# Two layers of attention and feed-forward on one core: who copies the last weight fold behind a branch, when Silu's table is loaded, and where two leftover value products stand

## The chip, the cores and the metric

The kernel runs on one core of a Trainium2 chip. The metric is the device time of one execution in microseconds (us), as the median over runs. The engines are named PE (TensorE), DVE (VectorE), ACT (ScalarE), POOL (GpSimd) and SP (SyncE, which issues most of the transfers).

## The reference

The input `x` is 8 x 100 x 512 and the context 8 x 361 x 128, all in float32. Two layers follow each other, each with an attention over the context and a feed-forward part:

```python
x = x + L0_xattn(layernorm(x), ctx)   # 16 heads of 32, causal mask, softmax
x = x + L0_ffn(layernorm(x))          # 8 experts, the best 2 per token, silu(x W1) * (x W2) W3
x = x + L1_xattn(layernorm(x), ctx)   # latent attention, 16 heads, rotated context, softmax over 361
x = x + L1_ffn(layernorm(x))          # weights, rows and hidden rounded to 8-bit steps, silu(gate) * up
```

In the second layer's attention the queries go through three weight matrices, `Wq`, `w_kc_q` and `W_qr`. They depend on no token, so the kernel multiplies them with each other once.

## The kernel before

The 800 tokens stand in seven tiles of 128 rows (the last has 32). The program is one long list of instructions for each engine. In most of it the order on PE, DVE and ACT is the order in which the program is written (`manual_schedule`); SP's and POOL's transfers are put in by a scheduler, which may also move them across a piece of code.

**The fold.** The product of the three weight matrices, `wqf`, is made in eight pieces, one for each pair of heads, beside the routing of the first layer. A piece goes through four steps: `fold_first` (two pieces at a time, small matmuls), `fold_turn` (two transposes by PE into a bank of PSUM, and a copy back into SBUF, L786), `fold_second` (matmuls with `Wq`, and a copy into the tile `f_p`, L796) and `fold_third` (four transposes of `f_p`, L802, and a copy into `wqf`, L803). All these copies are ACT's. The last pair of pieces is called `u4`: its `fold_first` and `fold_turn` stand ahead of the branch, its `fold_second` and `fold_third` behind it.

**The branch.** Each expert takes 240 tokens at most. If an expert has more, a slow loop of its own handles the rest; with these inputs it isn't entered. Each engine loads the flag `spilt` into a register (L1002) and skips the loop (L1009). Ahead of the branch POOL issues two indirect transfers that gather the rows of the first expert's tokens (`first_rows`, L906). On the skipped side POOL waits until both have landed and then raises the counters of its transfer queues by what the loop would have added; after that it gathers the rows of the second and third expert (`xg`).

**Behind the branch.** The order written out is: `fold_second` of both pieces of `u4`, `fold_third` of the first, `columns_of` (transposes of the gathered rows, L1128, in two parts of 128 and 112 rows; ACT copies the first part into `xgT`, L1132, DVE the second, L1130), `fold_third` of the second piece, and then the experts. An expert's matmuls of gate and up (L1191) read `xgT`. ACT applies Silu to the gate (L1202). A one-element Silu at L930, written into a corner of the tile `sd0`, stands at the end of the part ahead of the branch, so that the function's table is loaded early. `sd0` lies in a pool that is closed right behind it; the space is used again by the tiles into which SP loads the second layer's feed-forward weights (`gu`, L947, 256 KB each, and `dn`, L952, 704 KB), which DVE rounds beside the experts.

**The second layer's attention.** The work is cut into halves `(b, h)` of a batch, each with six tiles (`HT` is 6). A tile is a step: `scores(n)` (a matmul on PE, L1497, the row maximum `nm` on DVE, L1502, the exponential on ACT, L1505, into one of four buffers `e`), `scaled` (POOL divides by the sum, L1515) and `turned_squares` (DVE transposes squares of 32 x 32 into `sq`, L1522). Behind the six steps stands `values` of the half before (96 matmuls on PE, L1531, into the tile `four`, which takes four banks of PSUM and exists once).

Of 100 query rows 96 fit these tiles. The leftover rows of two batches and all heads make one tile of their own; it has its scores behind an even batch, and is finished in the second half of the next batch: `rest_columns` at step 2 (three transposes, L1546, into `four`, copied by ACT, L1548 and L1549) and `rest_values` at step 4 (six matmuls, L1558, into `four` again, copied by ACT into `ctxT`, L1563). A function put at a step by `at_step` is called ahead of this step's `scores`. There are four such halves.

Of the kernel before, what the change touches and what calls it, by code (L numbers as in the profile page):

```python
# [15 lines left out]
AF = mybir.ActivationFunctionType  # L16
# [3 lines left out]
P = 128  # L20
# [30 lines left out]
def tile_kernel(  # L51
# [7 lines left out]
    nc = tc.nc  # L59
# [19 lines left out]
    def bank(dtype=F32):  # L79
        cols = 512 if dtype == F32 else 1024  # L80
        bank_turn[0] += 1
        pool = bank_pools[bank_turn[0] % len(bank_pools)]
        return pool.tile([P, cols], dtype, tag="bank", name="bank")
# [15 lines left out]
    ln_eps = keep.tile([P, 1], F32, tag="ln_eps", name="ln_eps")  # L99
# [142 lines left out]
    sd0 = at.tile([P, NT], F32, tag="sd0", name="sd0")  # L242
# [527 lines left out]
    def fold_first(t_p, *pairs):  # L770
        pa = bank()
        for n, (i, wq_p, kq_p, qr_p) in enumerate(pairs):
            for c in range(CQ // P):
                for j in range(2):
                    nc.tensor.matmul(
                        pa[ds(R1 * j, R1), ts(n, P)], qr_p[:, j, c, :], kq_p[:, j, c, :],
                        start=(c == 0), stop=(c == CQ // P - 1),
                    )
        nc.scalar.copy(t_p, pa[:, : 2 * P])
        return [(i, wq_p) for i, wq_p, _, _ in pairs], t_p  # L780

    def fold_turn(pairs, t_p):
        pa = bank()
        for n in range(2):
            nc.tensor.transpose(pa[:, ts(n, P)], t_p[:, ts(n, P)], ident)
        nc.scalar.copy(t_p, pa[:, : 2 * P])  # L786
        return [(i, wq_p, t_p[:, ts(n, P)]) for n, (i, wq_p) in enumerate(pairs)]

    def fold_second(i, wq_p, a_p):
        pb = bank()  # L790
        for j in range(2):
            nc.tensor.matmul(
                pb[ds(R1 * j, R1), :], a_p[:, ts(j, R1)], wq_p[:, j, :], start=True, stop=True
            )
        f_p = fw.tile([P, D], F32, tag="f_p", name=f"f_p{i}", bufs=2)
        nc.scalar.copy(f_p, pb)  # L796
        return i, f_p

    def fold_third(i, f_p):
        pt = bank()  # L800
        for c in range(KC):
            nc.tensor.transpose(pt[:, ts(c, P)], f_p[:, ts(c, P)], ident)  # L802
        nc.scalar.copy(wqf[:, :, ts(i, P)], pt.rearrange("p (c r) -> p c r", c=KC))  # L803
# [43 lines left out]
    turned = at.tile([P, 2, 2 * P], F32, tag="zeros", name="turned")  # L847
    turned = [turned[:, 0], turned[:, 1]]
# [11 lines left out]
    token_scales(mvs, sd_all, rstd_all, 5, 7)  # L860
    u2 = fold_first(turned[1], loaded.pop(0), loaded.pop(0))
    u1 = fold_turn(*u1)
    nc.scalar.activation(sd0[:, 0:1], ln_eps, AF.Exp)
    for t in range(5, 7):
        gate_norm(t)
    mark_places(0, 5)
    u3 = fold_first(turned[2], loaded.pop(0), loaded.pop(0))
    u2 = fold_turn(*u2)
    f0 = fold_second(*u1[0])
    xT = gate_columns(5, 7)  # L870
    u3 = fold_turn(*u3)
    f1 = fold_second(*u1[1])
    name_tokens(0, 5)
    for i in (6, 7):
# [3 lines left out]
    add_tokens(0, 5)  # L878
    fold_third(*f1)
    f0 = fold_second(*u2[0])  # L880
    rank_choices(5, 7)
    f1 = fold_second(*u2[1])
# [10 lines left out]
    turned = fw.tile([P, 2 * P], F32, tag="a_p", name="turned3", bufs=1)  # L893
    u4 = fold_first(turned, loaded.pop(0), loaded.pop(0))
# [7 lines left out]
    def gather(e, tiles):  # L902
        got = []
        for i, xg in enumerate(tiles):
            n = SLOTS[i][1]
            d = nc.gpsimd.indirect_dma_start(  # L906
                out=xg, out_offset=None, in_=x_rows,
                in_offset=bass.IndirectOffsetOnAxis(
                    ap=token_of[:n, 2 * e + i : 2 * e + i + 1], axis=0
                ),  # L910
            )
            got.append((xg, d.ins))
        return got
# [7 lines left out]
    slots = {0: gather(0, first_rows)}  # L921
    most = small.tile([P, 1], F32, tag="most", name="most")
# [2 lines left out]
    nc.vector.tensor_scalar(spilt, most, float(CAP), None, ALU.is_gt)  # L925
    f3 = fold_second(*u3[1])
    fold_third(*f2)
    u4 = fold_turn(*u4)
    fold_third(*f3)
    nc.scalar.activation(sd0[:, 0:1], ln_eps, AF.Silu)  # L930
    close_atw()
    close_at()

# [174 lines left out]
    def choices(e, got):  # L1108
        gates = []
        for i, (xg, _) in enumerate(got):  # L1110
            n = SLOTS[i][1]
            one = ffw.tile([P, 1], F32, tag="one", name=f"one{e}_{i}", bufs=4)[:n]
            nc.vector.tensor_scalar(one, xg[:, D + 2 : D + 3], float(NE - e), None, ALU.is_equal)
            gate = ffw.tile([P, 1], F32, tag="gate", name=f"gate{e}_{i}", bufs=4)[:n]
            nc.vector.scalar_tensor_tensor(
                gate, xg[:, D : D + 1], one, xg[:, D + 1 : D + 2], ALU.mult, ALU.add
            )
            place = small.tile([P, 1], I32, tag="place", name=f"place{e}_{i}")[:n]
            nc.vector.tensor_copy(place, xg[:, D + 3 :])
            gates.append((gate, place))  # L1120
        return gates

    def columns_of(e, got):
        xgT = ffw.tile([P, KC, CAP], F32, tag="xgT", name=f"xgT{e}")
        for i, (s0, n) in enumerate(SLOTS):
            pt = bank().rearrange("p (c q) -> p c q", c=KC)
            for c in range(KC):
                nc.tensor.transpose(pt[:, c, :n], got[i][0][:, ts(c, P)], ident[:n, :n])  # L1128
            if i % 2:
                nc.vector.tensor_copy(xgT[:, :, ds(s0, n)], pt[:, :, :n])  # L1130
            else:
                nc.scalar.copy(xgT[:, :, ds(s0, n)], pt[:, :, :n])  # L1132
        return xgT
# [41 lines left out]
    )  # L1175
    in_order.__enter__()

    folded = [fold_second(*a) for a in u4]
    fold_third(*folded[0])
    turned = columns_of(0, slots[0])  # L1180
    fold_third(*folded[1])
    gates = choices(0, slots[0])

    for e in range(NE):
# [44 lines left out]
        if e + 1 < NE:  # L1229
            turned = columns_of(e + 1, slots[e + 1])  # L1230
# [18 lines left out]
        for m, i in down:  # L1249
            mr = HCH[m][1]  # L1250
            s0, n = SLOTS[i]
# [4 lines left out]
        for i in range(HC):  # L1256
            gate, place = gates[i]
            n = SLOTS[i][1]
# [181 lines left out]
    pairs, kvrs, kvTs, kv4s = {}, {}, {}, {}  # L1440
# [153 lines left out]
    for g, tiles in enumerate(GROUPS):  # L1594
        xT = xT_next
        n = sum(ROWS[t] for t in tiles)
# [52 lines left out]
    def at_step(k, i, f, *args):  # L1649
        beside.setdefault((k, i), []).append(lambda: f(*args))  # L1650

    for b in range(B):
        k = 2 * b
        at_step(k, 1, context_blocks, b, 0)
        at_step(k + 1, 0, context_blocks, b, 1)
        if b + 1 < B:
            at_step(k + 1, 0, next_columns, b + 1)
        if b % 2 == 0:
            at_step(k + 1, 0, next_rows, b)
            q = (k - 2, k) if b > 2 else (0, 1)  # L1660
            if b:
                for h in range(2):
                    at_step(q[h], 2 if q[h] else 5, queries, b, h, copies)
        else:
            n = first_of[b] - 1
            at_step(k + 1, 2, rest_columns, n)
            at_step(k + 1, 4, rest_values, n)

    turning = []

# [3 lines left out]
    for k, (b, h) in enumerate(halves):  # L1674
        n0 = first_of[b] + HT * h
        behind_rest = h == 0 and b % 2 == 1
        for i in range(HT):
            n = n0 + i
# [18 lines left out]
        if h and b % 2 == 0:  # L1697
            n = n0 + HT
# [364 lines left out]
```

## Time and profile before

| | |
|---|---|
| median of 3 runs | 624.99 us (624.87 to 627.96) |
| the profiled execution | 624.9 us, its span 622.7 us |
| granted TensorE clock, mean | 0.997 |
| PE busy (matmuls) | 601.0 us, 97% of the span |
| DVE, ACT, POOL busy | 403.5, 231.8, 238.8 us |
| the branch and what stands behind it, to the first expert's matmul | 132.8 to 140.2 us |
| experts | 140.2 to 261.3 us |
| second attention, steps and values | 321 to 484 us |

The span runs from the first to the last instruction; 2.2 us of the execution lie around it. Line numbers are those of the kernel before. A name such as `first_rows` or `four` is that of a tile in the program. In a row of a timeline the figures are the start, the duration, the engine, the line, the operation, the tiles, and in brackets the idle time of the engine ahead of it with the engine that ended it.

### The profile page before, as it was taken

Reading aid. Unit: us, or ns where it says so; the run is one execution under the profiler, and the core shown is the slowest. Engines: PE = TensorE matmul, PEld = TensorE weight load, DVE = VectorE, ACT = ScalarE, POOL = GpSimd, SP = SyncE. Lnnn points to the kernel's source line nnn. Section 1 sums busy time; section 2 is a strip of 40 time slices with the busy share of each in tenths; the row PEclk is TensorE's granted clock in tenths of the full one; section 3 lists DMA queues with packets and bytes.
Section 4 is the critical chain, followed back from the end, with each engine's and each line's share of the span. In section 5 each row is a group of like instructions: output and inputs, shape, how many; then the busy total and the mean of one; then the engine's idle time right before and its main releaser. Section 6 shows DMA issues by size and latency. Waiting matters only on the chain.

```text
span 622.7 us, 12244 instructions
## 1 busy us (share of the span) xinstructions
PE 601.0 (97%) x4587; PEld 399.4 (64%) x4594; DVE 403.5 (65%) x1041; ACT 231.8 (37%) x533; POOL 238.8 (38%) x242
## 2 busy tenths in 40 slices
PE   8999999979999999999999999999999999999995
PEld 5767765647777777658877677777777544444442
DVE  4865778836777554253227888788874366766687
ACT  3553545561111111241336545556553121222130
POOL 1131231021333332208954868688685001222020
PEclk9999999999999999999999999999999999999998
DMA  8900096558999999773623332433210401110221
GB/s 279 326 20 35 2 298 182 179 155 255 306 301 268 233 329 308 201 197 102 180 67 86 91 101 53 127 88 88 59 50 6 139 10 32 24 31 11 53 41 68
DMA packets 92932, 83.75 MB, mean 134 GB/s; under 512 B 41195, under 2 KB 69567, under 8 KB 92743
## 3 DMA queue, kind: packets, MB, share of 16 engines
q1 hardware_dynamic: 88775, 73.57, 41.3%
q0 software_dynamic: 4096, 9.38, 7.3%
q8 instruction: 37, 0.61, 0.4%
q14 instruction: 24, 0.20, 0.1%
HBM read 63.75 MB, written 12.36 MB: 122 GB/s over the span
## 4 chain that ended last, share of the span: by engine, by line
PE 69%; DVE 5%; ACT 2%; issue 1%; POOL 1%; ACTq 0%; DVEq 0%
PE bank L390 13%; PE bank L1191 12%; PE four L1531 11%; PE bank L1497 8%; PE bank L1614 7%; PE bank L1252 7%; PE bank L1789 3%; PE bank L1292 2%; PE four L1461 2%; PE bank L1128 1%; PE four L1558 1%; ACT e L1505 1%; DVE sq L1522 1%; POOL hid L1806 1%; PE bank L396 1%
## 5 line engine op out<-in xcount | busy, mean ns | idle before, releaser
L1515 POOL TENSOR_SCALAR e<-e,rs 128x361 f32<-128x361 f32 x96 | 113.0, 1192 | 41.1 <-DVE rs L1511 40.8
L390 PE MATMUL bank<-wvo,ctxT 128*128 128x512 f32 x192 | 84.4, 594 | 0.0
L1505 ACT ACTIVATE e<-bank,nm 128x361 f32<-128x361 f32 x100 | 56.5, 567 | 51.6 <-DVE rs L1511 43.5
L1191 PE MATMUL bank<-xgT,w 128*128 128x240 f32 (+1 forms) x384 | 74.1, 369 | 0.4 <-ACT xgT L1132 0.4
L1191 PEld LDWEIGHTS bank<-xgT,w 128*128 128x128 f32 (+1 forms) x384 | 64.7, 181 | 11.5 <-issue 6.2
L1502 DVE TENSOR_REDUCE nm<-bank 128x1 f32<-128x361 f32 x100 | 50.8, 509 | 27.1 <-PE bank L1497 19.0
L1531 PEld LDWEIGHTS four<-sq,kv 32*128 32x128 f32 (+1 forms) x1536 | 62.2, 185 | 8.4 <-issue 4.8
L1497 PE MATMUL bank<-kvT,qe 128*128 128x361 f32 x192 | 67.3, 483 | 0.2
L1531 PE MATMUL four<-sq,kv 32*128 32x192 f32 (+1 forms) x1536 | 66.9, 325 | 0.0
L1806 POOL TENSOR_TENSOR hid<-g,u 128x512 f32<-128x512 f32 (+1 forms) x17 | 20.4, 1216 | 112.1 <-ACT g L1797 110.5
L390 PEld LDWEIGHTS bank<-wvo,ctxT 128*128 128x128 f32 x192 | 36.0, 190 | 42.5 <-issue 41.8
L1522 DVE STREAM_TRANSPOSE sq<-e 128x384 f32<-128x384 f32 x96 | 53.6, 558 | 1.6 <-POOL e L1515 0.8
L1264 POOL DMA_INDIRECT x_acc<-y,place x16 | 25.1, 1570 | 75.6 <-ACT y L1263 45.1
L355 POOL TENSOR_TENSOR s<-s,rs 100x800 f32<-100x800 f32 x16 | 24.4, 1522 | 70.3 <-DVE rs L354 35.5
L1497 PEld LDWEIGHTS bank<-kvT,qe 128*128 128x128 f32 x192 | 33.4, 189 | 22.6 <-issue 5.7
L1252 PE MATMUL bank<-w,hT 128*128 128x512 f32 (+3 forms) x96 | 42.6, 593 | 0.0
L1614 PE MATMUL bank<-xT,wqf 128*128 128x256 f32 (+1 forms) x128 | 31.2, 394 | 0.0
L1252 PEld LDWEIGHTS bank<-w,hT 128*128 128x128 f32 (+3 forms) x96 | 17.0, 183 | 19.7 <-issue 15.6
L1789 PE MATMUL bank<-w1q,xqT 128*128 128x512 bf16 (+1 forms) x140 | 29.2, 361 | 0.2
L1614 PEld LDWEIGHTS bank<-xT,wqf 128*128 128x128 f32 x128 | 23.8, 190 | 5.3 <-issue 0.5
L1794 DVE SCALAR_TENSOR_TENSOR g<-bank,sx,swb 128x512 f32<-128x512 f32 (+1 forms) x18 | 12.6, 702 | 19.0 <-PE bank L1789 18.5
L1202 ACT ACTIVATE silu<-bank 128x240 f32<-128x240 f32 x16 | 5.9, 370 | 50.1 <-PE bank L1191 50.1
(296 smaller groups left out, 961.5 us busy)
## 6 DMA issues: line engine op xcount, KB each, us to landing
w<-in_w SPq DMA_DIRECT2D x8, 1408.0 KB
gu<-in_wgu SPq DMA_DIRECT2D x22, 256.0 KB
wq_p<-in_wq SPq DMA_DIRECT2D x8, 512.0 KB
w<-in_w SPq DMA_DIRECT2D x16, 256.0 KB
wo<-in_wo SPq DMA_DIRECT2D x8, 512.0 KB
kq_p<-in_wkcq SPq DMA_DIRECT2D x16, 192.0 KB
kv<-ctx_rot SPq DMA_DIRECT2D x32, 96.0 KB
dn<-in_wdn SPq DMA_DIRECT2D x4, 704.0 KB
```

The source lines that it names most:

```text
L390: nc.tensor.matmul(po[:, :D], lhs[:, c, ds(t * P, r)], rhs[:, c, :], start=(c == 0), stop=(c == chunks - 1),)
L1191: nc.tensor.matmul(po, w12_e[:, c, cols], xgT[:, c, :], start=(c == c0), stop=(c == c1 - 1))
L1252: nc.tensor.matmul(py[i][:n], hT[:mr, m, ds(s0, n)], w3_e[:mr, m, :], start=(m == blocks[0]), stop=(m == blocks[2]),)
L1497: nc.tensor.matmul(ps[:, :L], of_batch(b)[a][:, h, s].rearrange("p g q -> p (g q)"), kvTs[b], start=True, stop=True,)
L1502: nc.vector.tensor_reduce(nm, ps[:, :L], AX.X, ALU.max, negate=True)
L1505: nc.scalar.activation(e[:, :L], ps[:, :L], AF.Exp, bias=nm, accum_out=sm)
L1515: nc.gpsimd.tensor_scalar_mul(e[:, :L], e[:, :L], rs)
L1522: nc.vector.transpose(squares[b, h][:, a * (HT // 2) + s, :], e)
L1531: nc.tensor.matmul(pc[:, g, :cols].rearrange("p (t q) -> p t q", q=32), kv4s[b, j // NBH][ds(32 * g, n), j % NBH, :], eT[ds(32 * g, n), :, ...
L1614: nc.tensor.matmul(pq[:, i, :], wqf[:, c, ts(p0 + i, P)], xT[:, c, :], start=(c == 0), stop=(c == KC - 1),)
L1789: nc.tensor.matmul(pw[:r, :n], xqT[:, c, :r], w1q[:, c, ds(off, n)], start=(c == 0), stop=(c == KC - 1),)
L1806: nc.gpsimd.tensor_tensor(hid[:r, ds(c0, n)], g[:r, :n], u[:r, :n], ALU.mult)
```

## The change

It has three parts.

1. `fold_turn` of `u4` and the first `fold_second` of `u4` get DVE's copy instead of ACT's.
2. The one-element Silu goes from the end of the part ahead of the branch to the start of the part behind it, and writes `most` (a small tile that is not in the closed pool) instead of `sd0`. The second piece's `fold_third` goes between the two parts of `columns_of`.
3. `rest_values` goes from step 4 to step 5.

```diff
-    def fold_turn(pairs, t_p):
+    def fold_turn(pairs, t_p, copy=nc.scalar.copy):
...
-        nc.scalar.copy(t_p, pa[:, : 2 * P])
+        copy(t_p, pa[:, : 2 * P])
...
-    def fold_second(i, wq_p, a_p):
+    def fold_second(i, wq_p, a_p, copy=nc.scalar.copy):
...
-        nc.scalar.copy(f_p, pb)
+        copy(f_p, pb)
...
-    u4 = fold_turn(*u4)
+    u4 = fold_turn(*u4, nc.vector.tensor_copy)
     fold_third(*f3)
-    nc.scalar.activation(sd0[:, 0:1], ln_eps, AF.Silu)
...
-    def columns_of(e, got):
+    def columns_of(e, got, between=lambda: None):
...
         for i, (s0, n) in enumerate(SLOTS):
+            if i:
+                between()
...
-    folded = [fold_second(*a) for a in u4]
+    nc.scalar.activation(most, ln_eps, AF.Silu)
+    folded = [fold_second(*u4[0], nc.vector.tensor_copy), fold_second(*u4[1])]
     fold_third(*folded[0])
-    turned = columns_of(0, slots[0])
-    fold_third(*folded[1])
+    turned = columns_of(0, slots[0], lambda: fold_third(*folded[1]))
...
-            at_step(k + 1, 4, rest_values, n)
+            at_step(k + 1, 5, rest_values, n)
```

In the built program the order on the engines changes in these places, and in two more on SP's queue. The first two `gu` loads stand ahead of SP's branch, where they stood behind it: the tiles that they fill no longer wait for ACT's Silu in `sd0`. And in the second attention, one load of rotated context columns (`kvT`) stands ahead of the second part of a load of context rows (`kvr`), three times. On ACT there is one table load behind the branch, where there were two (ahead of L786's copy and at L930). DVE's copy of L786 stands ahead of DVE's branch.

## The prediction

> **What bounds the kernel now.** PE's matmuls fill 97% of the span, so a change pays only where PE stands idle, or where its work gets shorter (none does here). I first read the chain that ended last around the branch. From 133.7 to 137.8 us it isn't on PE:
>
> ```profile
> 133.70 1.28 ACT L786
> ...
> 135.00 0.37 ACT turned L786
> 135.37 0.49 ACT wqf L803
> ...
> 135.86 1.28 ACT L930
> ...
> 137.36 0.48 ACT f_p L796
> ...
> 137.89 0.66 PE bank L802 x4
> 138.54 0.82 PE bank L1128 x8
> 139.37 0.44 PE bank L802 x4
> ...
> 140.18 1.86 PE bank L1191 x8
> ```
>
> ACT loads a table, copies, loads the next table, and PE's last fold hangs on it. The timeline of PE gives what PE lost: 1.20 us at the branch itself, 0.95 ahead of L792 (for `turned`), 0.53 ahead of L802 (for `f_p`), 0.38 ahead of L1191 (for `xgT`). The change is aimed at the 0.95 and the 0.53.
>
> Next the transfers there, in the timeline of POOL and the two tiles' views (from issue to landing):
>
> ```profile
> 131.27 1.23 POOL L906 DMA_INDIRECT first_rows<-x_rows,token_of  x1 [31.90 <-DVE spilt L925]
> 132.81 0.96 POOL L906 DMA_INDIRECT first_rows<-x_rows,token_of  x1 [0.31 <-PE bank L802]
> 138.56 0.96 POOL L906 DMA_INDIRECT xg<-x_rows,token_of  x1 [4.79 <-PE bank L802]
> ...
> DMA to landing us min/median/max: 4.6/4.6/4.6
> ...
> DMA to landing us min/median/max: 5.8/6.4/6.7
> ```
>
> The first rows landed at 131.27 + 4.6 = 135.9 and 132.81 + 4.6 = 137.4, the later gathers (`xg`) took 5.8 to 6.7. Third, SP's waits there and DVE's queue ahead of its `xgT` copy (the view of L1130):
>
> ```profile
> SPq L947 <- ACT sd L930: 4.9, 1, 4.9
> ...
> L1130 DVEq EVENT_SEMAPHORE  x8: 49/50/1064, 137.7 to 138.3; - x8
> ```
>
> SP held the `gu` loads 4.9 us for the Silu into `sd0`. DVE's eight waits ahead of L1130 begin at 137.7, just behind the second landing: POOL raises its queues' counters only then. Last, the waits of the second attention:
>
> ```profile
> PE four L1558 <- ACT rest L1549: 2.3, 4, 0.6
> ```
>
> Four times PE stands 0.45 to 0.62 us for the copies of the leftover columns.
>
> **The branch, on PE.** PE's first matmul behind it stays at 133.96: DVE's new copy waits for PE's transposes (over at 132.5) and takes at most the 0.62 of L1130's larger copy, so it ends by 133.2; behind it on DVE stand only the branch and a copy that isn't wanted before 135.4. Three L802 end at 134.47. `turned` is ready, so L792 follows at once: eight instructions in 1.94 us, half of them at 135.45 and all at 136.42. DVE's copy of `f_p` is priced by L1296 (128x512 out of PSUM, 0.69): over at 136.2, under the second half. Then four L802 (0.66) to 137.1, four transposes of rows (half of 0.98) to 137.5, four L802 (0.44) to 138.0, four transposes to 138.4. ACT's copy of the second `f_p` (0.58, from 136.5) is covered, and so is its one table load (133.7 to 135.0). What the new order costs: DVE's `xgT` copy (0.62) now stands behind the last transposes with no L802 over it, and with the hand-overs on both sides (0.1 each) L1191 starts at 139.2. Sum: 140.18 - 139.2 = 1.0 us won, 0.95 + 0.53 less some 0.45.
>
> **The branch, on the transfers.** There is a second way to L1191. From the second landing to DVE's first wait it is 0.26, the other seven waits take 0.78 (0.1 each) up to the copy, then 0.62 and 0.1: landing plus 1.8. With 137.4 that is 139.2 too. So behind the change both ways end together, and each tenth by which the gather lands later is lost on PE.
>
> It will land later. With the Silu out of `sd0`, the `gu` loads don't wait, and two stand ahead of SP's branch. SP is ready at 137.39 - 4.9 = 132.5, so three times 256 KB and 704 KB start some 5 us earlier, on top of the gathers. The windows show the transfer engines 0.69, 0.83, 0.46 busy in 133 to 136 with the gathers alone, and 1.0 in 139 to 140 with the loads. Bounds for the second gather: 4.6 (loads cost nothing) and 6.7 (the worst `xg`), so L1191 at 139.2 or at 132.81 + 6.7 + 1.8 = 141.3: 1.0 us won to 1.1 us lost. I take 5.4: the loads came to their full rate some 1.6 us behind their first issue, which puts it at 134, when the first gather is mostly through; the second runs under them, but stands behind the first in its queue and not behind a full backlog, as `xg` did. That is L1191 at 140.0, and 0.2 us won. From there on PE has no gap over 0.15 us until the attention, so it arrives undiminished.
>
> Two rules of the Trainium skill differ from rows here. L786's copy starts 0.01 us behind the end of its table load of 1.28. "ScalarE: Activation LUTs" (What ACT_TABLE_LOAD costs) counts 1.28 for the load and 1.38 for a drain, 2.66 for a switch; with it ACT's second `f_p` copy would end at 137.6, and the gain on PE's way would be some 0.2 smaller. "DMA: Bandwidth & Descriptors" (Rules for kernel authors) says to issue transfers early so that their fixed cost hides under compute; by that the earlier loads are free, the branch gives 1.0 and the total is 623.7. The rows of 4.6 and 5.8 say otherwise.
>
> **The attention.** At step 4 the fourth score matmul issues its last part at 354.80, and L1558 starts at 355.72, bound by ACT's copy that ends at 355.67. The change puts the fifth score (two parts of 0.30) into this hole, so L1558 stays at 355.72, and PE would come to `values` 0.61 us earlier, four times: 2.4 us. But `values` writes `four`, the one tile that L1563's two copies still read, and in the order on ACT these copies now stand behind the fifth exponential. Until now they came ahead of it, 357.31 to 357.64, under the two scores. The fifth exponential needs its row maximum on DVE: behind the transposition that ends at 356.96, 0.51 long and overlapped by 0.07, so over at 357.4; the hand-over is 0.1 and the exponential starts at 357.5. A copy follows 0.55 behind an exponential's start (354.59 to 355.14), and the two take 0.33: over at 358.36. `values` starts at 358.41, where it was 358.47. So the wait moves from L1558 to L1531 and 0.06 is left; the other three halves have the same spacing on DVE and ACT. Sum: 4 x 0.06 = 0.2 us. Bounds: the whole 2.4, and below nothing, one more transposition (0.56) ahead of the maximum, 4 x 0.5 = 2.0 lost; the built order shows one transposition only, so I stay at 0.2. What is queued behind the later copies on ACT, the sixth exponential, waits for a score that is itself earlier. On SP a `kvT` load now stands ahead of part of `kvr`: each issue takes 0.4, its wait ends with the sixth score some 1 us later, and the rows are read two halves on (37 us). Nothing.
>
> **Sum.** 624.9 (the profiled execution: 622.7 of span and 2.2 around it; the median of the runs is 0.1 above it) - 0.2 - 0.2 = 624.5.
>
> **The rivals.** *The loads don't collide* (landing at 4.6): 624.9 - 1.0 - 0.2 = 623.7. For it: the two gathers leave the transfer engines a third free. Against: the `xg` rows. *Slower, by the collision*: the second gather takes 6.7 as the worst `xg` did; 1.1 lost, 0.2 won, 625.8. It decides from a landing 1.2 us later than now on. For it: the loads are issued within 1 us of the first gather's issue and fill the engines. Against: `xg` stood in a queue of four. *The attention's wait goes whole*, if L1563's copies get in ahead of the exponential or `values` needn't wait for them: 624.9 - 0.2 - 2.4 = 622.3. Against it is ACT's written order. *The change doesn't do what it says* at one place: the table is loaded once, but ACT's time there was not the only limit.
>
> **How the numbers follow.** The forecast (gather late by 0.4 to 1.2, attention nearly nothing; 624.1 to 624.9 by itself) 0.5; loads harmless 0.2; slower 0.2; attention whole 0.1. The first three span 623.7 to 625.8; with half of the attention's 2.4 beside harmless loads 622.6, and with 0.4 for a gather worse than any seen 626.2: the range, with about 1 in 10 left out. About 0.5%, 3.1 us, is what a measurement of this kernel can tell from no change. To win that, harmless loads and the whole attention must meet (621.5): 0.05. To lose it, the worst gather and the attention's lower bound: 0.05. Within: 0.9.
>
> **What would show it.** In the profile after: one table load behind the branch; PE without the 0.95 and 0.53 gaps; `gu` issued near 132.5; `first_rows` landing over 4.6, and the gap ahead of the first expert's matmul grown by as much over 0.8; no PE wait at `rest_values`, but one of some 0.5 us ahead of `values`, released by ACT's `ctxT` copy. Wrong would be: `first_rows` still at 4.6; no wait ahead of `values`; or a new wait of PE in the experts.

## The result, and the profile after

The changed kernel takes 628.75 us (median of 11 runs) beside 624.95 for the kernel before on the same chip: a ratio of 1.0052, interval 1.0037 to 1.0068. That is slower, at the edge of what can be told from no change, and outside the range of 622.6 to 626.2. (Now and then an execution of any of these kernels takes 630 us and more at a lower clock; the ratios leave out those told apart as disturbed.) The profiled execution of the changed kernel took 626.45 us, its span is 624.7 us at a clock of 0.997, and it is the shortest of the eleven. So there are two questions: where do 1.5 us of the profile come from, and where the 2.3 us more of the median?

Line numbers behind L930 differ from those of the kernel before: L1129 are the rows' transposes, L1192 the first expert's matmul, L1532 `values`, L1564 the copy into `ctxT`, and L946 and L951 the `gu` and `dn` loads. PE's timeline behind the branch:

```profile
133.91 0.52 PE L802 MATMUL bank<-ident,f_p 128*128 128x128 f32 x3 [1.25 <-PEq L1008]
134.37 1.94 PE L792 MATMUL bank<-wq_p,turned 128*64 128x512 f32 x8
136.24 0.66 PE L802 MATMUL bank<-ident,f_p 128*128 128x128 f32 x4
136.73 0.60 PE L1129 MATMUL bank<-ident,first_rows 128*128 128x128 f32 x4
137.17 0.60 PE L802 MATMUL bank<-ident,f_p 128*128 128x128 f32 x4
139.75 0.60 PE L1129 MATMUL bank<-ident,first_rows 112*128 112x112 f32 x4 [1.97 <-DMA first_rows<-x_rows,token_of]
141.49 1.86 PE L1192 MATMUL bank<-xgT,w 128*128 128x240 f32 x8 [1.14 <-DVE one L1112]
```

The two waits for ACT are gone, and PE is done with the fold's last transposes at 137.8, where the sum had 138.0. Then it stands 1.97 us for the second part of the gathered rows. The last row's 1.14 us are the way on from there; the profile names a small instruction of DVE (L1112) as what ended it, but what L1192 reads is DVE's copy into `xgT` just ahead of it, from 140.76 to 141.39. The first expert starts at 141.49 where it started at 140.18. SP's timeline and the view of the tile `first_rows` (issue to landing, least, median, most) show why:

```profile
132.36 1.22 SPq L946 DMA_DIRECT2D gu<-in_wgu  x3
133.63 0.43 SPq L951 DMA_DIRECT2D dn<-in_wdn  x1
```

```profile
  PE bank L1129: 2.0, 1
...
DMA to landing us min/median/max: 4.4/5.7/7.0
```

Three `gu` loads and a `dn` load (1.47 MB together) are issued 5 us earlier than before, and the second gather takes 7.0 us instead of 4.6. It was issued at 132.67, landed at 139.7, and L1192 follows 1.8 us behind. The windows of one us show the crowd (behind the length of the window come the busy times of PE, its weight loads, DVE, ACT and POOL, with numbers of instructions; the last three columns are the granted clock, the busy share of the transfer engines, and GB/s):

```profile
135.00:136.00 1.00, 1.00 (x8) 0.16 (x2) 0.51 (x1) 0.53 (x2) 0.00 (x0) 1.00 1.02 389
136.00:137.00 1.00, 1.00 (x9) 0.76 (x8) 0.18 (x1) 0.60 (x2) 0.00 (x0) 1.00 1.06 373
137.00:138.00 1.00, 0.77 (x8) 0.53 (x5) 0.00 (x0) 0.52 (x1) 0.00 (x0) 1.00 1.10 339
138.00:139.00 1.00, 0.00 (x0) 0.00 (x0) 0.00 (x0) 0.00 (x0) 0.00 (x0) 1.00 0.92 305
```

The same windows of the kernel before, where the gathers had the engines to themselves and were over at 137.4:

```profile
135.00:136.00 1.00, 0.58 (x4) 0.29 (x6) 0.00 (x0) 1.00 (x3) 0.00 (x0) 1.00 0.46 161
136.00:137.00 1.00, 1.00 (x8) 0.19 (x4) 0.00 (x0) 1.00 (x1) 0.00 (x0) 1.00 0.06 17
```

The rest is in PE's waits of the changed kernel (total, times, longest):

```profile
PE four L1532 <- ACT ctxT L1564: 1.8, 4, 0.5
...
PE bank L1846 <- DMA xqT<-xq: 0.7, 1, 0.7
...
PE bank L1253 <- DVE hT L1216: 0.3, 1, 0.3
```

Set against the kernel before, PE's instructions run 1.31 us late at L1192, and another 0.45 at L1253 near 201 us, where DVE had waited for a `dn` load that landed 8.6 us after its issue. Near 274 us 0.2 is won back. Each half of the attention with leftovers wins 0.66 at the scores behind `rest_values` and gives 0.58 back at `values`: 0.3 over four halves. Near 500 us 0.73 are lost to the transfer of `xqT`. That last one goes with the execution and not with the change: of two profiles of one and the same kernel ("loads_free" and "loads_free2" below) the first has no such wait and the second 1.0. The ends of the two spans lie 2.0 apart.

### The profile page after: what moved, and what is told of

It is laid out like the page before. It is cut to its first block, busy times and chain, and to the rows that moved or that the text cites. A ratio compares the mean times of both kernels' runs of the same rounds, so it can differ in the third digit from the quotient of the medians.

```text
span 624.7 us, 12251 instructions
## 1 busy us (share of the span) xinstructions
PE 601.9 (96%) x4594; PEld 399.5 (64%) x4594; DVE 405.2 (65%) x1043; ACT 229.5 (37%) x530; POOL 239.3 (38%) x242
## 4 chain that ended last, share of the span: by engine, by line
PE 74%; DVE 11%; DMA 7%; ACT 3%; issue 2%; POOL 1%; SPq 1%; DVEq 0%; ACTq 0%; POOLq 0%
PE bank L390 13%; PE four L1532 11%; PE bank L1192 10%; PE bank L1615 7%; PE bank L1498 7%; PE bank L1253 5%; PE bank L302 4%; PE bank L1790 3%; DMA dn<-in_wdn 3%; PE bank L1293 2%; PE four L1462 2%; DVE sq L1523 2%; DMA wq_sb<-in_wq 1%; DMA swb<-scale_row 1%; DVE nm L1503 1%
## 5 line engine op out<-in xcount | busy, mean ns | idle before, releaser
L1192 PE MATMUL bank<-xgT,w 128*128 128x240 f32 (+1 forms) x384 | 74.1, 369 | 1.1 <-DVE one L1112 1.1
L1192 PEld LDWEIGHTS bank<-xgT,w 128*128 128x128 f32 (+1 forms) x384 | 64.7, 181 | 12.2 <-issue 6.2
L1532 PEld LDWEIGHTS four<-sq,kv 32*128 32x128 f32 (+1 forms) x1536 | 62.2, 185 | 10.5 <-ACT ctxT L1564 4.1
L1532 PE MATMUL four<-sq,kv 32*128 32x192 f32 (+1 forms) x1536 | 67.0, 325 | 1.8 <-ACT ctxT L1564 1.8
L1253 PE MATMUL bank<-w,hT 128*128 128x512 f32 (+3 forms) x96 | 42.9, 594 | 0.3 <-DVE hT L1216 0.3
L1253 PEld LDWEIGHTS bank<-w,hT 128*128 128x128 f32 (+3 forms) x96 | 16.9, 183 | 20.4 <-issue 15.3
L1790 PEld LDWEIGHTS <-xqT 128*128 128x128 bf16 x144 | 13.8, 98 | 16.6 <-DMA xqT<-xq 2.1
```

The costliest lines, as they stand in the source:

```text
L1192: nc.tensor.matmul(po, w12_e[:, c, cols], xgT[:, c, :], start=(c == c0), stop=(c == c1 - 1))
L1253: nc.tensor.matmul(py[i][:n], hT[:mr, m, ds(s0, n)], w3_e[:mr, m, :], start=(m == blocks[0]), stop=(m == blocks[2]),)
L1532: nc.tensor.matmul(pc[:, g, :cols].rearrange("p (t q) -> p t q", q=32), kv4s[b, j // NBH][ds(32 * g, n), j % NBH, :], eT[ds(32 * g, n), :, ...
L1790: nc.tensor.matmul(pw[:r, :n], xqT[:, c, :r], w1q[:, c, ds(off, n)], start=(c == 0), stop=(c == KC - 1),)
```

## Experiments

The theory: the early loads share the transfer engines with the second gather, and all else is as forecast. The rival: DVE's copies or the new order cost the time.

**loads_free: the early loads alone**

```diff
 # kernel before
-    nc.scalar.activation(sd0[:, 0:1], ln_eps, AF.Silu)
+    nc.scalar.activation(most, ln_eps, AF.Silu)
```

> The kernel before, with the one-element Silu of L930 written into `most` instead of `sd0`; all copies, orders and the attention stay. Theory (the loads run into the gathers): `gu` is issued near 132.5 us, the second `first_rows` gather takes about 7.0 us (7.03 in the changed kernel) and lands near 139.7, L1191 starts at landing + 1.8 = 141.5 instead of 140.18, and the time is 1.3 us or more above the kernel before (626.2). Rival (DVE's copies and the new order on PE make the loss): gather 4.6 us, L1191 at 140.2, 624.9 us. On the clock: if a longer wait of PE behind the branch lowers the granted clock in the timed runs, it is under 0.997 here, and the median is 2 us worse than the profile's own sum.

Measured: 625.45 us, ratio 1.0008 (0.9996 to 1.0021). The gather took 6.1 us, and L1191 started 6.75 us behind PE's return from the branch instead of 6.22. The direction is the theory's, the size is not: 0.5 us on PE, and nothing that the times can tell from no change. Mean clocks were 0.994 to 0.999, much as those of the kernel before.

**held: the changed kernel without the early loads**

```diff
 # changed kernel; the loads' calls stand behind `folded = ...`
         w = ...
+        if held:
+            nc.scalar.copy(w[:, 0:1], ln_eps)   # gu0, gu1, gu2, dn0
         nc.sync.dma_start(w, ...)
```

> The changed kernel, with the first three `gu` loads and the first `dn` load held by one-element writes of ACT into their tiles, behind ACT's copy of the second `f_p` (137.1 us). Theory (collision): the second gather takes 4.6 us again, L1192 starts at 139.2 to 139.5, 0.7 to 1.0 us ahead of the kernel before, and with the attention's 0.2 to 0.3 the time is 623.6 to 624.0. Rival (the copies and the order): a wait of over 1 us stays ahead of L1192, and the time is 626 or more.

Measured: 623.82 us beside 625.2, ratio 0.9984 (0.9975 to 0.9994): the gain forecast for harmless loads. The tile's view and PE's timeline:

```profile
DMA to landing us min/median/max: 3.5/4.2/4.8
```

```profile
137.63 0.55 PE L1133 MATMUL bank<-ident,first_rows 112*128 112x112 f32 x4
139.27 2.06 PE L1196 MATMUL bank<-xgT,w 128*128 128x240 f32 x9 [1.10 <-DVE one L1116]
```

The gather takes 4.8 us, the rows wait for nothing, and the first expert (here L1196) starts at 139.27; the prediction had 139.2 for both of its ways. The rival is out: copies, table and order are all still in this kernel. What is left, 1.10 us ahead of L1196, is the way from the landing.

**attn_only** and **branch_only: the two halves of the change**

```diff
 # attn_only: kernel before
-            at_step(k + 1, 4, rest_values, n)
+            at_step(k + 1, 5, rest_values, n)
 # branch_only: changed kernel
-            at_step(k + 1, 5, rest_values, n)
+            at_step(k + 1, 4, rest_values, n)
```

> The kernel before with `rest_values` at step 5 and nothing else. Theory: the four waits of 0.45 to 0.62 us ahead of `rest_values` go, and four of 0.45 come ahead of `values`, released by ACT's second copy into `ctxT`; 0.06 to 0.08 us won each time, 624.6 us. Rival (the attention's part is where the changed kernel loses beyond its branch): 2 us or more above the kernel before, 627.

> The changed kernel with `rest_values` back at step 4: DVE's copies, the moved Silu and the order behind the branch alone. Theory: L1192 at 141.5, and the loss of the profiled execution of the changed kernel is here whole, 1.5 to 2.0 us (626.7), with the rest of its median (628.7) only if the granted clock falls under 0.997. Rival (the two parts hurt each other): under 0.5 us lost here.

Measured: attn_only 624.34 beside 625.2, ratio 0.9987 (0.997 to 1.0005), with the moved wait in the place and size expected (four times 0.45 ahead of `values`). branch_only 628.25, ratio 1.0065 (1.004 to 1.009): the loss is all in the branch. Its profile (627.66 us) has what the changed kernel's profile had not. Windows of branch_only:

```profile
138.00:142.00 4.00, 1.57 (x9) 1.34 (x10) 1.31 (x7) 1.07 (x2) 1.27 (x2) 1.00 0.18 65
142.00:145.00 3.00, 3.00 (x9) 2.52 (x8) 0.00 (x0) 0.00 (x0) 2.39 (x3) 0.50 0.76 193
145.00:146.00 1.00, 1.00 (x5) 0.89 (x4) 0.00 (x0) 0.00 (x0) 0.11 (x1) 0.79 0.65 215
```

PE had waited 2.49 us for the rows (the gather took 7.5) and 1.14 for `xgT`, with 0.60 of work between. One us after it took up the expert its granted clock was 0.50 for 3 us and 0.79 for one: 1.5 + 0.2 = 1.7 us of work lost. That is 0.0027 of the span, just what separates a mean clock of 0.995 from 0.998. Of the ten executions of the changed kernel that its ratio counts nine had 0.995 or less, and only the profiled one 0.997. So the pause is paid twice, if this is what the median holds.

The mean clock tells such executions apart only roughly, because it is also 0.50 at the very end, behind PE's last matmul, for a time that differs (1.2 us of the span in the profile of "filled" below, 4.2 in the changed kernel's). The profiles without a fall in between have means of 0.997 to 0.999, the four with a single one of 3.4 us 0.995 or 0.996.

**filled: the pause filled with work**

```diff
 # changed kernel, first expert only
+            for _ in range(16 if i and e == 0 else 0):      # ahead of L1129's second part
+                nc.tensor.transpose(pt[:, 0, :], ident, ident)
...
+            for _ in range(8 if e == 0 and m == blocks[0] else 0):   # ahead of L1192
+                nc.tensor.transpose(pw[:, :P], ident, ident)
```

> The changed kernel with PE kept at work while it waits: sixteen transposes of the identity ahead of the second part of the rows' transposes (L1129) and eight ahead of the first expert's matmul (L1192), into the banks that are overwritten right behind; what they write is used by nothing. The loads stay early. Theory (the pause of PE costs twice: once as a wait for the gather, once as a granted clock of 0.50 in the 3.4 us behind it, seen in one trace of two): the gather still takes 7 us and L1192 still starts near 141.5, but no slice behind it shows a lower clock, and the median falls from 628.7 by about 1.7 us to 626.4 to 627.0, with mean clocks of 0.996 and more. Rival (the rest of the median's loss is not from the pause): the median stays within 0.5 us of 628.7, the clocks at 0.993 to 0.995.

Measured: 627.34 us, ratio 1.0044 (1.0011 to 1.0078). Ten of twelve executions had clocks of 0.997 to 0.999 (the two others, at 633.5 and 635.4 us, widen the ratio); the clock followed the theory. The filling isn't complete: PE still stood 1.16 us for the rows and 0.27 for `xgT`. The gather took 7.9 us, and the median is higher than the 626.4 to 627.0 expected. By its ratio alone this kernel can't be told from the changed one (1.0052), so the two were run again, side by side on one chip.

> The changed kernel itself, beside the filled one on the same chip. If the early loads always cost this order of work a late gather: 6.8 to 7.9 us for the second one, L1192 1.3 to 2.8 us later than in the kernel before, the clocks 0.995 or less in most executions, the median 628 to 629.5. If the gather's delay is by chance: 5.7 to 6.1 us as in the kernel before with the early loads.

> The changed kernel with transposes of the identity in PE's two pauses behind the branch, as in the filled run. Theory (the pause costs a second time, through the clock): clocks of 0.997 and more, and a median 1.2 to 2.0 us under that of the changed kernel in the same call. Rival (the fall of the clock isn't what the timed runs lose): within 0.5 us of it.

Measured: after_again 629.45, ratio 1.0062 (1.0036 to 1.0087), every clock 0.996 or less; filled_again 627.27, ratio 1.0015 (0.9995 to 1.0035), nine of twelve clocks 0.997 or more. The medians lie 2.2 us apart, though the filled kernel's gather took 7.8 us and the other's 7.0. In after_again's profile the clock falls too, behind pauses of 1.96 and 1.14 us. The changed kernel's first profile has the same two pauses (1.97 and 1.14) without a fall, so it takes more than their length. Windows of after_again:

```profile
141.00:142.00 1.00, 1.00 (x3) 0.87 (x4) 0.44 (x5) 0.00 (x0) 0.69 (x2) 0.50 0.22 37
142.00:143.00 1.00, 1.00 (x4) 0.81 (x4) 0.00 (x0) 0.00 (x0) 0.69 (x2) 0.50 0.74 235
143.00:144.00 1.00, 1.00 (x4) 0.87 (x3) 0.00 (x0) 0.00 (x0) 0.69 (x2) 0.50 0.75 186
144.00:145.00 1.00, 1.00 (x6) 0.91 (x6) 0.00 (x0) 0.00 (x0) 0.89 (x1) 0.95 0.66 128
```

The same windows of filled_again:

```profile
143.00:144.00 1.00, 1.00 (x7) 0.94 (x6) 0.04 (x1) 0.00 (x0) 0.93 (x1) 1.00 0.63 120
144.00:145.00 1.00, 1.00 (x7) 0.94 (x6) 0.00 (x0) 0.00 (x0) 0.73 (x1) 1.00 0.68 194
```

Work without use, put into a wait, makes the kernel faster: that is the second price of the pause. The two intervals only just stay apart (1.0036 and 1.0035). (after_again's profiled execution was a long one, 634.5 us. There `dn` loads took 9.5 us to land, PE stood 0.9 us near 187 and 3.2 near 206 for DVE's `hT`, and the clock fell a second time, for some 7 us.)

**dn_held, two_gu, one_gu: how many of the loads it takes**

```diff
 # held, with the hold taken off some loads
-load_gate_up(gate_up_left.pop(0), held=True) for _ in range(GB)
+load_gate_up(gate_up_left.pop(0)) for _ in range(GB)               # dn_held
+load_gate_up(gate_up_left.pop(0), held=i > 1) for i in range(GB)   # two_gu
+load_gate_up(gate_up_left.pop(0), held=i > 0) for i in range(GB)   # one_gu
```

> The changed kernel with only the first `dn` load (704 KB) held behind ACT's copy of the second `f_p`; the three `gu` loads (768 KB together) stay early. If the bytes queued behind the gather decide, half the bytes give half the delay: a gather of 5.5 to 6 us, L1192 near 140.3, and 625 us. If the `gu` loads, issued ahead of the gather's own landing, do it all: 7 us and 141.5 as in the changed kernel. If `dn` does it all: 4.6 to 4.8 and 139.3, 624.0.

> The changed kernel with the third `gu` load and the first `dn` load held; two `gu` loads of 256 KB stay early, those that stand ahead of SP's branch. With the bytes: about 6.1 us of gather, L1192 near 140.6. If only what is issued behind the second gather (the third `gu`, `dn`) delays it: 4.8 and 139.3.

> The changed kernel with the second and third `gu` load and the first `dn` load held behind ACT's copy of the second `f_p`; only one `gu` load of 256 KB stays early. If the delay of the second gather goes with the bytes that are queued around it, it lies between the 4.8 us of no early load and the 6.8 of three: about 5.5 us, L1192 near 140.0. If one early load is enough for the whole delay: 6.8 and 141.3.

The tile's view of the three, in the order one_gu, two_gu, dn_held (the largest number is the second gather):

```profile
DMA to landing us min/median/max: 4.4/4.7/5.1
```

```profile
DMA to landing us min/median/max: 4.5/5.3/6.1
```

```profile
DMA to landing us min/median/max: 4.7/5.7/6.8
```

With no early load 4.8, with one of 256 KB 5.1, with two 6.1, with three 6.8, with `dn` as well 7.0 to 7.9. The middle three are single profiles, and profiles with the same loads differ: with all loads held 4.6, 4.8 and 5.2 (best, held and best_filled), with all four early 0.9 apart. So one load can't be told from none; that two and more delay the gather is clear, the size of each step is not. For dn_held the second alternative came nearest: half of the bytes made most of the delay. They are issued around the gather, `dn` a us behind it. two_gu came out at the 6.1 forecast by bytes, one_gu under the 5.5. In both L1196 follows the landing by 1.7 to 1.8 us. The times: dn_held 630.06, ratio 1.0049 (1.0013 to 1.0085), so holding `dn` alone wins nothing; two_gu and one_gu were executed once each, at 633.4 and 635.4 us, with the long `dn` waits near 200 us of after_again, and say nothing on the time.

**loads_free2: is it the order?** The same edit as loads_free.

> The kernel before with the moved Silu write alone, a second look: in the first one SP's issue of the third `gu` load took 1.34 us instead of 0.33 to 0.43, and the gather took 6.1 us. If that late issue spared the gather, an ordinary issue here goes with a gather of 6.8 to 7.9 and a wait ahead of L1191 of 1.3 to 2.3 us; if the order of PE and ACT of the kernel before spares it, the gather takes about 6.1 again with ordinary issues.

Measured: SP's issue of the third `gu` took 0.79, of `dn` 0.43, and the gather 5.7 us (625.6 us). The issue was much shorter than the 1.34 of loads_free and the gather no longer, which speaks against a late issue as what spared it; but 0.79 isn't an ordinary issue either, so this isn't decided. With the order of the kernel before, the same four loads cost 1.1 to 1.5 us of gather, with the changed order 2.4 to 3.3. Why is open. The packets tell that with the order before the loads' data began to move 0.5 and 1.1 us behind the second gather's issue, and in the five profiles with the changed order 1.3 to 1.5; what sets this is not shown, and two profiles against five may not be enough to exclude chance. In this profile the clock fell as well, to 0.50 for 3.4 us from 134.2 on, behind the branch's pause of 1.20 us and in the 0.95 ahead of L792.

**split, best, best_filled: the attention without its new wait, and a faster kernel**

```diff
 # kernel before
-            at_step(k + 1, 4, rest_values, n)
+            at_step(k + 1, 4, products_ahead, first_of[b] + HT + 4)   # the fifth score's matmul
+            at_step(k + 1, 4, rest_values, n)
...
-        ps = bank()
+        ps = ahead.pop(n, None) or score_products(n)
```

> The kernel before; at step 4 only the fifth score's matmul is put ahead of `rest_values` on PE, while on ACT the copies into `ctxT` stay ahead of the fifth exponential. Theory (ACT's order moved the wait): neither `rest_values` nor `values` waits, and 0.45 to 0.6 us are won four times, 1.8 to 2.4 us, 622.8 us. Rival (`values` is bound by something else there, its squares from DVE or POOL): PE waits ahead of `values` as in the changed kernel, 624.6.

Measured: 623.32 us beside 625.88, ratio 0.996 (0.9932 to 0.9988). PE runs 0.60 to 0.64 us earlier four times, 2.5 in all, and waits at neither place. PE's timeline of split:

```profile
355.61 1.99 PE L1502 MATMUL bank<-kvT,qe 128*128 128x361 f32 x6
357.43 1.55 PE L1568 MATMUL four<-rest,kvr 121*128 121x64 f32 x12
358.82 0.83 PE L1502 MATMUL bank<-kvT,qe 128*128 128x361 f32 x2
359.58 2.72 PE L1541 MATMUL four<-sq,kv 32*128 32x192 f32 x60
```

and of the changed kernel:

```profile
358.69 0.83 PE L1498 MATMUL bank<-kvT,qe 128*128 128x361 f32 x2
359.97 2.23 PE L1532 MATMUL four<-sq,kv 32*128 32x192 f32 x48 [0.46 <-ACT ctxT L1564]
```

PE's order is the same in both; only ACT's two copies stand ahead of an exponential instead of behind it. Split has the branch of the kernel before, and in its profile the clock fell there too, behind pauses of 1.20 and 0.94 us with 0.52 of work between. Windows of split:

```profile
136.00:139.00 3.00, 3.00 (x10) 0.76 (x7) 0.00 (x0) 2.26 (x5) 0.28 (x1) 0.56 0.20 51
139.00:140.00 1.00, 1.00 (x8) 1.00 (x7) 0.00 (x0) 0.60 (x2) 0.69 (x2) 0.62 0.79 293
```

So the kernel before pays this as well, in about half of its executions: in the four sets in which it ran beside others, 15 of 27, 15 of 32, 5 of 15 and 7 of 19 had a clock of 0.995 or less. These were 1.2, 1.6, 2.3 and 0.7 us slower, on average, than those of the same set with 0.997 or more. The held kernel, whose pauses lie 4.3 us apart, had none under 0.996 in eleven.

> The changed kernel with the loads held (as in the run with held loads) and with the attention's order of the split run. Theory: both gains add, 0.8 at the branch and 1.8 to 2.4 in the attention, 621.8 to 622.4 us, faster than both kernels. Rival (what is won in the attention is given back at its end, in the transfers of the scales): 623.5 or more.

> The changed kernel with the loads held and the split attention, and with eight transposes of the identity in the 1.1 us that PE waits ahead of L1192 (their product is overwritten). Theory (PE's pauses of 1.20 and 1.10 with 3.7 us of work between them still let the granted clock fall in some executions): no clocks of 0.994 are left, and the median is 0.3 to 0.8 us under that of the same kernel without them (622.5), 621.7 to 622.2. Rival (the pause at the branch alone does it, or these pauses do nothing): 622.5 with the same spread of clocks.

best puts `held` and `split` together; best_filled adds the eight transposes ahead of the first expert. Measured: best 622.79, ratio 0.9951 (0.9929 to 0.9973); best_filled 622.45, ratio 0.994 (0.9918 to 0.9962). Both beat both kernels. best misses its 621.8 to 622.4 by 0.4, best_filled its 621.7 to 622.2 by 0.25. Of the executions that the ratios count, two of best's ten had a clock of 0.994, and none of best_filled's nine was under 0.997. So pauses 4.3 us apart (the expectation's 3.7 is too low) still let the clock fall now and then, if these two mean a fall. The clocks agree with the theory, but two of ten against none of nine can be chance, and the difference of the times is within their intervals.

## Why the prediction was wrong, by its own steps

**Right: PE's way behind the branch.** `turned` was ready, L792 ran at 134.37, DVE's copy of `f_p` was over at 136.18 (136.2 in the sum), `gu` was issued at 132.36 (132.5). Without the transfers it ends at 139.27, where the sum had 139.2.

**Right: the second way.** Landing plus 1.8 us held in every kernel in which the landing came last (1.79 in the changed kernel, 1.74 in two_gu).

**Wrong, the term that failed: "I take 5.4" for the second gather.** It was 7.0, and 7.0 to 7.9 in the other profiles with the same loads and order, over the bound of 6.7. The reason given, that the gather "stands behind the first in its queue and not behind a full backlog", mistook what it shares: not the queue but the engines, which are full from 135 to 139. The bound was taken from the later gathers, though the bytes could have been added up: the two gathers and the four loads are 2.0 MB, and the rate with all engines busy was 300 to 390 GB/s, which makes an estimate of five to seven us. (It doesn't tell the 5.7 of loads_free2 from the 7.9 of filled; that is the open part.) So 0.2 won at L1192 became 1.3 lost. The slower rival named the right mechanism with a gather too short: 6.7 us in it, 7.0 in the profile and up to 7.9 in others.

**Wrong by leaving it out: the clock.** The sum counted all of PE's work behind a wait at full speed. In the profiles in which it fell the clock was halved for some 3.4 us behind the pause, 1.7 us that no row of the profile before showed. By the mean clocks the kernel before pays them too, in about half of its executions, and the changed one in nearly all. "TensorE: Matmul & The Clock Gate" (Part 1: The HAM clock gate) of the Trainium skill gives half rate after at least one idle window of some 3.4 us, and says that the window runs free. The 3.4 us and the change from execution to execution fit the runs here; that the window has to be idle does not: PE had worked 0.60 us in the middle of branch_only's 4.2, and 0.52 in the 2.7 of split. In both this work was transposes, the kind that kept the clock up where it filled the pause, so it isn't that such work doesn't count.

**Right: the attention.** Forecast 0.06 four times, measured 0.08, with the new wait where it was put. Split shows that the reason, ACT's written order, was the right one: 0.6 four times when it is turned.

**Smaller: "it arrives undiminished".** Between the branch and the attention 0.45 more was lost, to a `dn` load that landed late, and 0.2 of it won back.

**What this adds up to.** The profiled execution is 1.95 us over the forecast of 624.5: 1.5 for the gather's term, 0.3 for the `dn` load and 0.7 for `xqT`, less some 0.5 (1.75 us lie around its span, where it was 2.2, and the attention won 0.1 more). The median lies 2.3 above the profile. One fall of the clock is 1.7 of that; the rest, 0.6, is not told apart. Five of the ten executions have clocks of 0.992 or 0.993, lower than a single fall gave in any profile, and no trace here shows where they lost more. (A slip that decides nothing: 624.9 - 1.0 - 1.2 is 622.7 and not the 622.6 at the lower end of the range.)

**The rules cited.** The prediction took "DMA: Bandwidth & Descriptors" (Rules for kernel authors) to say that the early loads are free, for a total of 623.7; the rule speaks of the fixed cost alone. That total came out, as 623.8, when the loads were held back; with early loads it was 628.75. The drain of 1.38 us that "ScalarE: Activation LUTs" counts isn't in this trace either: the one table load ends at 134.84, the Silu starts at 134.85, and ACT's second `f_p` copy ends at 136.99, not at 137.6.

## What to carry to other kernels

A wait that seems to serve nothing may hold transfers back: before taking it away, list what is queued behind it on every queue, and price their bytes against what is in flight, at the rate that the windows show. If the wait was useful, put it back where it is wanted: four one-element copies of 0.19 us on an idle engine did it. A pause of PE may cost a second time through the clock, so look at the mean clock of every execution, not of the profiled one alone.

## What the runs showed of the hardware

- The granted clock was 0.50 for some 3.4 us behind two pauses of PE close together (2.49 and 1.14 us around 0.60 of work in branch_only; 1.20 and 0.94 around 0.52 in split; in loads_free2 from the middle of the second of such a pair on), in some executions and not in others. Transposes of an identity matrix in the pause kept it at 1.00 in both profiles.
- Behind single waits of 3.19, 4.83 and 6.59 us near 200 us (after_again, two_gu, one_gu) it was 0.50 for some 7, 7 and 10 us, from 2.6 to 2.7 us into the wait on.
- The same four loads lengthened the same gather from 4.6 to anything between 5.7 and 7.9 us.
